# C and GpSimd's B loaded from a copy in DRAM, and the second stage's norms by transposes with VectorE's statistics

## The chip, the cores and the metric

The kernel runs on one core of a Trainium2 chip. The metric is the device time of the whole program in microseconds, the median of several runs; one more execution is profiled, and every busy time and wait below is from that one. A core has five engines that work through their own instruction streams in order and wait for each other by semaphores: TensorE (PE, with its weight loads shown apart as PEld), VectorE (DVE), ScalarE (ACT), GpSimd (POOL) and SyncE (SP), which here issues nearly all DMA transfers.

## The reference

Four layers follow each other on an image batch x of shape (4, 192, 64, 64), all in float32. Layers 0 and 1 hold the selective scans, and are what the change concerns:

```python
# layer 0: tokens = 4096 rows of 192 values per image
xs = layernorm(x); out = xs + mamba1(xs) + mamba2(flip(xs, channels))
# layer 1: t = layernorm over channels of each position
x1 = x + mamba(t);  x2 = x1 + gelu(batchnorm(depthwise3x3(x1)))
out = x2 + mlp(layernorm(x2))            # 192 -> 768 -> gelu -> 192

def mamba(x):                            # d = 384 inner channels, n = 16 states
    xc, z = split(x @ in_w.T)
    xc = silu(causal_conv(xc))
    dt, B, C = split(xc @ x_w.T)         # 12, 16 and 16 values per token
    dt = softplus(dt @ dt_w.T + dt_b)
    h[t] = exp(dt[t] * A) * h[t-1] + (dt[t] * xc[t]) * B[t]     # for each d and n
    y[t] = sum_n h[t] * C[t] + D * xc[t]
    return (y * silu(z)) @ out_w.T
```

Layer 2 is a depthwise convolution with weights made from the image's means, layer 3 a window transformer with a 16-fold structured product. The change leaves both alone.

## The kernel before, in words

The program has three stages. `two_mambas` does layer 0 (to about 5160 us), `mamba_block` layer 1 (to about 8480 us), `conv_and_windows` layers 2 and 3. In the first two stages an image is cut into 8 tiles of T = 512 tokens, 32 tiles in all. A mamba on a tile is 12 groups k of 4 scans j: the 384x16 states lie as 48 pieces of 128 partitions (16 channels by 8 states), and each piece is one scan of 512 steps on VectorE. Stage one has two mambas a tile, so 96 scans; stage two one, so 48.

For each group, `load` (L598) brings dt and dt*xc from DRAM, each row repeated over 8 partitions (dtE and dtxE, 4 transfers of 256 KB each). `product` (L635) multiplies dtxE by B: VectorE for most groups, with B in PSUM, and GpSimd for the groups named `shared`, with a copy Bs of B in SBUF. `decay` (L647) makes dA = exp(dtE * A) on ACT into one of three PSUM banks, two scans ahead. `step` (L653) is the scan on VectorE. `read` (L664) keeps the last state and multiplies h by C on GpSimd. `sum` (L672) adds over the states by four matmuls on TensorE.

B and C are needed with each of their 16 rows repeated over the partitions. In the kernel before this is a matmul of the tile `dbl` (the 44 values per token) with a matrix of ones (`Expand.spread`): `spread` (L607) for B, `spread_C` (L616) for C, whose result ACT copies to SBUF (L630), as it copies B for GpSimd (Bs). C0 has one buffer in stage two (`alone`), otherwise C has two; Bs has one.

Around the scans stands everything else of a tile. `front` (L464) is the input projection, the convolution, `dbl` (L496), dt, and the writes of dt and dt*xc to DRAM (`r_dt`, `r_dtx`, L520). In stage two, `norm` is the layernorm before it, `back` (L1076) the output projection with the residual into `strip`, `tail` (L1120) the 3x3 convolution (ps_dw), a Gelu, an addition and a second layernorm, and `end` the MLP. These are generators in five lanes of `Behind` (L176). Once per scan, `tick` lets lanes emit a `Piece` each, as far as its declared cost fits: `pe` against a budget of TensorE time per scan, `act` against one of ACT time, `bank` against two PSUM banks, `after` against flags, `wait` against a number of scans, `burst` only where VectorE is about to do a product (long ACT operations with a table load), `lock` one norm at a time. `later` emits an evacuation one to three scans after its matmul. So the order on each engine is fixed when the program is built, by the planner's counts, and the engines then run as semaphores let them. Tiles' `norm` runs two tiles ahead of the scan, `front` one tile ahead, `tail` one or two behind.

The second stage's norms (`NormT.run`, L303) work with channels in partitions. A matmul with a matrix of 1/192 gives the mean in every partition, VectorE subtracts it (L310), ACT squares (L317), 8 matmuls with one output column each give the variance (L322), ACT and GpSimd make the reciprocal root (L333, L334), 4 matmuls spread it (L340), VectorE multiplies (L348), and ACT applies gain and shift (L355).

All transfers named here are issued from SP's queue in program order. Each waits there for its source, for its buffer to be free, and for an older transfer, and holds those behind it.

Of the kernel before, what the change touches and what calls it, by code (L numbers as in the profile page):

```python
# [286 lines left out]
class NormT:  # L287


    FIRST = dict(pe=1.7, bank=True)  # L290

    def __init__(self, nc, const, work, behind):
        self.nc, self.work, self.behind = nc, work, behind
        self.mean_w = const.tile([CP, CP], F32, name="mean_w")
        nc.vector.memset(self.mean_w, 1.0 / C)
        self.eps = const.tile([128, 1], F32, name="eps")
        nc.vector.memset(self.eps, EPS)
        self.minus_half = const.tile([128, T // 128], F32, name="minus_half")
        nc.vector.memset(self.minus_half, -0.5)
        self.ident = const.tile([128, 128], F32, name="ident")  # L300
        make_identity(nc, self.ident)

    def run(self, x, g, b, d, which):  # L303
        nc, behind = self.nc, self.behind
        nq = T // 128
        mean = behind.bank([CP, T], "mean")
        for k in range(2):
            nc.tensor.matmul(mean, self.mean_w, x[:, k, :], start=(k == 0), stop=(k == 1))
        h = behind.later(
            lambda: nc.vector.tensor_tensor(  # L310
                d, x, mean.unsqueeze(1).broadcast_to([CP, 2, T]), ALU.subtract
            ),
            dve=True,
        )
        yield Piece(after=[h], wait=3, act=1.05, lock=True)
        sq = self.work.tile([CP, 2, T], F32, name="ln_sq", bufs=1)
        nc.scalar.activation(sq, d, AF.Square)  # L317
        yield Piece(2.5, wait=2, bank=True)
        var = behind.bank([128, nq], "var")
        for q in range(nq):  # L320
            for k in range(2):
                nc.tensor.matmul(  # L322
                    var[:, q : q + 1],
                    sq[:, k, bass.ts(q, 128)],
                    self.mean_w[:, 0:1],
                    start=(k == 0),
                    stop=(k == 1),
                )
        behind.locked = False
        rs = self.work.tile([128, nq], F32, name="ln_rs", tag=f"ln_rs{which}", bufs=1)  # L330

        def power():
            nc.scalar.activation(rs, var, AF.Identity, bias=self.eps)  # L333
            nc.gpsimd.tensor_tensor(rs, rs, self.minus_half, ALU.pow)  # L334

        h = behind.later(power, act=0.25)
        yield Piece(1.3, after=[h], wait=4, bank=True)
        rb = behind.bank([CP, T], "rb")
        for q in range(nq):
            nc.tensor.matmul(  # L340
                rb[:, bass.ts(q, 128)],
                rs[:, q : q + 1].to_broadcast([128, CP]),
                self.ident,
                start=True,
                stop=True,
            )
        h = behind.later(
            lambda: nc.vector.tensor_tensor(  # L348
                d, d, rb.unsqueeze(1).broadcast_to([CP, 2, T]), ALU.mult
            ),  # L350
            dve=True,
        )
        for k in range(2):
            yield Piece(after=[h], wait=0 if k else 3, act=0.8)
            nc.scalar.activation(  # L355
                d[:, k, :], d[:, k, :], AF.Identity, scale=g[:, k : k + 1], bias=b[:, k : k + 1]
            )
# [49 lines left out]
class Expand:  # L407
# [5 lines left out]
    def __init__(self, nc, const, spread_ap, gather_ap):  # L413
        self.spread = const.tile([KX, 4, 128], F32, name="spread")
        nc.sync.dma_start(self.spread, spread_ap)
        self.gather = const.tile([128, 2, 32], F32, name="gather")
        nc.sync.dma_start(self.gather, gather_ap)


class Mamba:  # L420
# [43 lines left out]
    def front(self, xn, first, u):  # L464
# [26 lines left out]
        yield Piece(2.6, bank=True, wait=2 if self.summed else 4)  # L491
# [6 lines left out]
        for d in range(ND):  # L498
            yield Piece(0.85, bank=True, after=[h], wait=0 if d else 3)
            if d == 0:  # L500
                dt = self.work.tile([128, ND, 1 + T if self.summed else T], F32, name="dt", bufs=1)
                dt = dt[:, :, :T]
                dtx = raw[:, :, K - 1 :]
# [103 lines left out]
    def spread(self, u, o):  # L607

        B = u["B", o] = self.psum_a.tile([128, T], F32, name=f"B{o}", bufs=1)
        self.nc.tensor.matmul(B, self.ex.spread[:, o, :], u["dbl"], start=True, stop=True)  # L610

# [4 lines left out]
    def spread_C(self, u, o):  # L616

        both = [("Bs", 0, 1)] if any(k % 2 == o for k in self.shared) else []
        both.insert(len(both) if self.summed else 0, ("C", 2 + o, 1 if self.alone(o) else 2))
        for n, i, bufs in both:  # L620
            if n == "C":
                yield Piece(0.85, bank=True, wait=3 * self.alone(o))
            v = self.work.tile([128, T], F32, name=f"{n}{o}", bufs=bufs)
            if n == "C":
                ps = self.behind.bank([128, T], f"ps_{n}")
                self.nc.tensor.matmul(ps, self.ex.spread[:, i, :], u["dbl"], start=True, stop=True)
            else:
                ps = u["B", o]
            done = self.behind.later(
                lambda v=v, ps=ps: self.nc.scalar.copy(v, ps), bank=(n == "C")  # L630
            )
            yield Piece(after=[done])
            u[n, o] = v

# [75 lines left out]
class Scans:  # L710
# [6 lines left out]
    def __init__(self, nc, units, behind):  # L717
        self.nc, self.units, self.behind = nc, units, behind
        self.due = {}
        for n, unit in enumerate(units):  # L720
# [3 lines left out]
            unit[1]["z_free"] = [units[n - 2][1]["gated"]] if n > 1 else []  # L724

# [287 lines left out]
def mamba_block(tc, x, p96, p96_ap, p128, p128_ap, m_in, ex_aps, out, sums, following):  # L1013
# [4 lines left out]
    with ExitStack() as ctx:  # L1018
# [50 lines left out]
        def norm(u):  # L1069
            xn = u["xn"] = scan.tile([CP, 2, T], F32, name="xn", bufs=1)  # L1070
            yield from ln.run(u["x"], w["ln1_g"], w["ln1_b"], xn, 1)
# [48 lines left out]
        def tail(b, t):  # L1120
# [37 lines left out]
            yield Piece(1.7, bank=True, wait=4, after=[taken[0]])  # L1158
            xn = work.tile([CP, 2, T], F32, name="xn2", tag="xn2", bufs=1)
            yield from ln.run(x2, w["ln2_g"], w["ln2_b"], xn, 2)  # L1160
            units[b * NT + t]["past"][0] = True
            taken[0] = [False]
            behind.add(3, end(b, t, x2, xn, taken[0]), Piece(1.7, bank=True, wait=2))
# [28 lines left out]
        def before(n):  # L1192
            if n + 1 < len(units):
                behind.add(1, front(units[n + 1]), Piece())
            if n + 2 < len(units):
                behind.add(1, norm(units[n + 2]), Piece(1.7, bank=True, after=[units[n + 2]["loaded"]]))

        def after(n):
# [3 lines left out]
            first = [u["done"]] + ([units[n - 3]["ended"]] if n > 2 else [])  # L1202
            for t2 in ([t - 1] if t else []) + ([t] if t == NT - 1 else []):
                behind.add(2, tail(b, t2), Piece(2.6, bank=True, after=first, wait=2))
# [7 lines left out]
        behind.add(1, norm(units[0]))  # L1212
        behind.add(1, front(units[0]), Piece())
        behind.add(1, norm(units[1]))
# [523 lines left out]
def scan_matrices():  # L1738
    spread = np.zeros((KX, 4, 16, 8), np.float32)
    for o in range(4):  # L1740
        for n in range(8):
            spread[RK + 8 * o + n, o, :, n] = 1.0
# [4 lines left out]
    return spread.reshape(KX, 4, 128), gather.reshape(128, 2, 32)  # L1747
# [100 lines left out]
```

## Time and profile before

| | |
|---|---|
| median of 3 runs | 10454.71 us (10451.56 to 10456.62) |
| profiled execution, its time | 10458.36 us |
| its span | 10456.3 us |
| granted TensorE clock, mean | 0.87 |
| busy over the span: PE, DVE, ACT, POOL | 81%, 84%, 64%, 76% |
| DMA | 1515.56 MB, mean 145 GB/s |
| L655, scans on VectorE | 4608, 1.27 us each |
| L668, L642, GpSimd's products with C and Bs | 1152 and 320, 4.53 and 4.58 us each |
| L630, ACT's copies of C and Bs | 192 and 128, 0.58 and 0.59 us each |
| L626, matmuls for C | 384 records, 223.6 us |
| L308, L322, L340, matmuls of the norms | 148.4, 140.1, 81.9 us |

Times are microseconds from the start of the span. A busy time is the time in which an engine worked on instructions of a group; the idle time beside it is that just before them, with the engine and line whose work ended it. Idle time of an engine that sets no pace costs nothing. A float32 matmul of this kernel leaves two records, a transpose one. Matmuls overlap, so their mean duration is longer than the share of busy time of each.

### The profile page before, as it was taken

The numbers are of one execution on the slowest core, as the hardware profiler recorded it, in microseconds if no ns is written. First come the engines' busy times: TensorE is split into PE (matmuls) and PEld (weight loads), VectorE is DVE, ScalarE is ACT, GpSimd is POOL, SyncE is SP. The second block draws the span as 40 slices with busy tenths as digits, with TensorE's granted clock in tenths as the row PEclk, the third lists the DMA queues.
The fourth block names the chain that finished last, engine by engine and source line by source line (L and its number), as shares of the span: only waits on it lengthen the run. The fifth ranks groups of instructions, "written<-read, shape, count | busy, mean of one in ns | idle before, by whom it ended". The sixth has DMA issues, their size and how long they took to land. (4 is left out here: it accounts for less than half of the span.)

```text
span 10456.3 us, 96737 instructions
## 1 busy us (share of the span) xinstructions
PE 8434.2 (81%) x30648; PEld 3477.0 (33%) x30648; DVE 8762.8 (84%) x7569; ACT 6672.4 (64%) x9690; POOL 7925.1 (76%) x3712
## 2 busy tenths in 40 slices
PE   6777777777777777777658898888898886989898
PEld 2222322222222222222223333333333333545455
DVE  7999999999999999999958888888888876555552
ACT  5777777767766767677646777777777753444433
POOL 6999999999999999999959888888888861101100
PEclk8888888888888888888768899999999997999999
DMA  6666666666666666666645555555555543122110
GB/s 166 177 183 185 181 182 182 182 179 182 184 183 179 182 185 183 179 183 185 160 120 154 150 141 151 146 151 147 146 156 139 152 109 74 44 61 53 41 41 19
DMA packets 969737, 1515.56 MB, mean 145 GB/s; under 512 B 244308, under 2 KB 277280, under 8 KB 968712
## 3 DMA queue, kind: packets, MB, share of 16 engines
q1 hardware_dynamic: 968224, 1506.06, 54.7%
q8 instruction: 243, 3.98, 0.2%
q10 hardware_dynamic: 1000, 3.30, 0.1%
q14 instruction: 270, 2.21, 0.1%
HBM read 1295.91 MB, written 213.12 MB: 144 GB/s over the span
## 5 line engine op out<-in xcount | busy, mean ns | idle before, releaser
L655 DVE TENSOR_TENSOR_SCAN h<-dA,m_state,h 128x512 f32<-128x512 f32 x3328 | 4040.0, 1266 | 219.9 <-ACT dA L649 157.6
L649 ACT ACTIVATE dA<-dtE,m_A 128x512 f32<-128x512 f32 x4608 | 3103.8, 686 | 1236.2 <-DVE h L655 939.8
L668 POOL TENSOR_TENSOR h<-h,C 128x2048 f32<-128x2048 f32 x832 | 3768.6, 4530 | 71.2 <-ACT C L630 3.7
L642 DVE TENSOR_TENSOR h<-dtxE,B 128x2048 f32<-128x2048 f32 x832 | 1882.4, 2262 | 79.1 <-DMA dtxE<-r_dtx 69.0
L655 DVE TENSOR_TENSOR_SCAN h_apart<-dA,m_state,h_apart 128x512 f32<-128x512 f32 x1280 | 1551.6, 1263 | 143.8 <-ACT dA L649 136.7
L642 POOL TENSOR_TENSOR h_apart<-dtxE,Bs 128x2048 f32<-128x2048 f32 x320 | 1464.7, 4577 | 20.5 <-ACT dA L649 10.7
L668 POOL TENSOR_TENSOR h_apart<-h_apart,C 128x2048 f32<-128x2048 f32 x320 | 1449.5, 4530 | 25.8
L677 PE MATMUL y<-h,gather 128*32 128x512 f32 x6656 | 1040.9, 702 | 428.4 <-POOL h L668 242.8
L1383 POOL TENSOR_TENSOR d<-d,rs 128x512 f32<-128x512 f32 x64 | 86.4, 1350 | 1596.2 <-DVE rs L1382 1576.1
L476 PE MATMUL ps_in<-xT,m_in_w 96*128 96x512 f32 x1536 | 951.6, 772 | 340.2 <-ACT o L919 213.4
L558 PE MATMUL ps_conv<-raw,m_conv 128*128 128x512 f32 x1536 | 724.3, 601 | 25.8 <-ACT raw L483 19.0
L476 PEld LDWEIGHTS ps_in<-xT,m_in_w 96*128 96x128 f32 x1536 | 365.6, 248 | 933.3 <-issue 372.7
L494 PE MATMUL ps_x<-xc,m_pack 128*68 128x512 f32 x576 | 374.8, 802 | 213.3 <-ACT xc L490 198.6
L1132 PE MATMUL ps_dw<-strip,dw 96*96 96x512 f32 x1152 | 544.8, 620 | 1.3 <-ACT x L1141 0.9
L677 PE MATMUL y<-h_apart,gather 128*32 128x512 f32 x2560 | 395.5, 694 | 171.9 <-POOL h_apart L668 161.1
L505 PE MATMUL ps_dt<-dbl,m_dt_w 68*128 68x512 f32 x576 | 379.3, 761 | 167.6 <-ACT dbl L496 101.3
L677 PEld LDWEIGHTS y<-h,gather 128*32 128x32 f32 x6656 | 140.3, 115 | 1072.1 <-issue 574.0
L1548 PE MATMUL sed_ps<-xn,sed 64*128 64x256 f32 (+3 forms) x2944 | 486.1, 403 | 7.0 <-DVE y L1567 7.0
L476 PE MATMUL ps_in<-xn,m_in_w 96*128 96x512 f32 x768 | 393.8, 647 | 118.2 <-ACT z L483 65.0
L396 PE MATMUL ps_o<-hid,t 128*96 128x512 f32 x768 | 412.9, 676 | 76.6 <-ACT C L630 69.2
L515 POOL TENSOR_TENSOR raw<-dt,xc 128x1536 f32<-128x1536 f32 x96 | 324.8, 3384 | 176.6 <-ACT dt L514 130.5
L649 ACT ACT_TABLE_LOAD x345 | 442.6, 1283 | 14.7 <-DMA dtE<-r_dt 8.6
(200 smaller groups left out, 11998.0 us busy)
## 6 DMA issues: line engine op xcount, KB each, us to landing
dtE<-r_dt SPq DMA_DIRECT2D x2304, 256.0 KB, 5.3
dtxE<-r_dtx SPq DMA_DIRECT2D x2304, 256.0 KB, 4.4
r_dt<-dt SPq DMA_DIRECT2D x96, 768.0 KB, 4.0
r_dtx<-raw SPq DMA_DIRECT2D x96, 768.0 KB, 6.5
x<-x SPq DMA_DIRECT2D x64, 384.0 KB, 3.6
img<-x SPq DMA_DIRECT2D x28, 512.0 KB, 9.1
xt<-in_x SPq DMA_DIRECT2D x32, 384.0 KB, 5.2
x<-o SPq DMA_DIRECT2D x32, 384.0 KB, 3.8
```

The costliest lines, as they stand in the source:

```text
L396: nc.tensor.matmul(ps, self.w2[:, m, bass.ts(k, CP)], h[:, m, :], start=(m == 0), stop=(m == NH - 1),)
L476: nc.tensor.matmul(ps, self.in_w[:, k, bass.ts(e, 128)], xn[:, k, :], start=(k == 0), stop=(k == 1))
L494: nc.tensor.matmul(ps, self.x_w[:, d, :], xc[:, d, :], start=(d == 0), stop=(d == ND - 1))
L505: nc.tensor.matmul(ps, self.dt_w[:, bass.ts(d, 128)], dbl, start=True, stop=True)
L558: nc.tensor.matmul(ps, self.conv[:, d, j, :], raw[:, d, j : j + T], start=(j == 0), stop=(j == K - 1))
L642: engine.tensor_tensor(h, u["rows", k // 2, 1], u[B, k % 2].unsqueeze(1).broadcast_to([128, 4, T]), ALU.mult)
L649: self.nc.scalar.activation(dA, u["rows", k // 2, 0][:, j, :], AF.Exp, scale=self.A[:, k, j : j + 1])
L655: self.nc.vector.tensor_tensor_scan(h[:, j, :], u.pop(("dA", k, j)), h[:, j, :], self.state[:, k, j : j + 1], ALU.mult, ALU.add,)
L668: nc.gpsimd.tensor_tensor(h, h, u["C", k % 2].unsqueeze(1).broadcast_to([128, 4, T]), ALU.mult)
L677: self.nc.tensor.matmul(u["ys"][32 * j : 32 * j + 32, :], self.ex.gather[:, i // 2, :], h[:, j, :], start=(i == 0), stop=(i == 3 and self. ...
L1132: nc.tensor.matmul(ps, dw[:, k, j, :], s[:, k, dy : dy + rows, dx : dx + HW], start=(j == 0), stop=(j == 8),)
L1548: nc.tensor.matmul(out, sed[p, int(h is not None), i ^ position(k, s), cols], xn[b, g][p, c, :], start=group(t) not in begun, stop=left[gr ...
```

## The change

- `front` writes the 32 rows of B and C of `dbl` to DRAM (`r_bc`), just before the dt projection.
- `spread_C` no longer uses TensorE, PSUM or ACT: C and Bs come by one transfer each of 256 KB from `r_bc`, in which every row is read 16 times. B for VectorE stays a matmul into PSUM. The matrix `spread` shrinks from four parts to two.
- A flag `spread`, set when the second half of B is spread, now holds the next `dbl` back (`dbl_free`).
- `NormT.run` turns the tile around: 8 transposes on TensorE to tokens in partitions (ln_t), two copies on ACT (ln_xs), `bn_stats` and `bn_aggr` for four groups of 128 tokens on VectorE, four small operations on GpSimd (with the reciprocal root), four scalings on ACT, 8 transposes back (ln_b), and gain and shift on ACT as the evacuation. The output tile is taken only at the transposes back, by the function `to`; the wait for the MLP before (`taken`) moves there too. The lock is taken with the first piece and kept to the last transposes.
- The tail waits for the end of the MLP two tiles before its own tile, written so that it also holds at an image's last tile.

```diff
 class NormT:
-    FIRST = dict(pe=1.7, bank=True)
+    FIRST = dict(pe=0.5, bank=True, lock=True)
...
-    def run(self, x, g, b, d, which):
...
+    def run(self, x, g, b, to, which, after=()):
+        nc, behind, ident = self.nc, self.behind, self.ident
         nq = T // 128
...
+        xs = self.work.tile([128, nq, C], F32, name="ln_xs", bufs=1)
+        made = []
+        for part in range(0, nq, 2):
+            if part:
+                yield Piece(0.5, bank=True)
+            ps = behind.bank([128, 2, C], "ln_t")
+            for q in range(2):
+                for k in range(2):
+                    nc.tensor.transpose(
+                        ps[:, q, bass.ts(k, CP)], x[:, k, bass.ts(part + q, 128)], ident[:CP, :CP]
+                    )
+            made.append(
+                behind.later(lambda part=part, ps=ps: nc.scalar.copy(xs[:, part : part + 2, :], ps), act=0.5)
+            )
+        yield Piece(after=made, wait=3)
...
+        for q in range(nq):
+            nc.vector.bn_stats(sums[:, q].rearrange("p a b -> p (a b)"), xs[:, q, :])
+        for q in range(nq):
+            nc.vector.bn_aggr(mv[:, q, :], sums[:, q].rearrange("p a b -> p (a b)"))
+        yield Piece(wait=1)
+        nc.gpsimd.tensor_scalar(rs, mv[:, :, 1], EPS, None, ALU.add)
+        nc.gpsimd.tensor_tensor(rs, rs, self.minus_half, ALU.pow)
+        nc.gpsimd.tensor_tensor(shift, mv[:, :, 0], rs, ALU.mult)
+        nc.gpsimd.tensor_scalar(shift, shift, -1.0, None, ALU.mult)
+        yield Piece(wait=3)
+        for q in range(nq):
+            yield Piece(act=0.55)
+            nc.scalar.activation(
+                xs[:, q, :], xs[:, q, :], AF.Identity, scale=rs[:, q : q + 1], bias=shift[:, q : q + 1]
+            )
         for k in range(2):
...
+            yield Piece(0.5, bank=True, wait=0 if k else 2, after=after)
+            out = out if k else to()
+            ps = behind.bank([CP, T], "ln_b")
+            for q in range(nq):
+                nc.tensor.transpose(ps[:, bass.ts(q, 128)], xs[:, q, bass.ts(k, CP)], ident)
+            h = behind.later(
+                lambda k=k, ps=ps, out=out: nc.scalar.activation(
+                    out[:, k, :], ps, AF.Identity, scale=g[:, k : k + 1], bias=b[:, k : k + 1]
+                ),
+                act=0.75,
+            )
         behind.locked = False
...
+        yield Piece(after=[h])
@@ front
-        yield Piece(2.6, bank=True, wait=2 if self.summed else 4)
+        yield Piece(2.6, bank=True, wait=2 if self.summed else 4, after=u["dbl_free"])
...
             if d == 0:
+                bc = u["bc"] = self.dram.tile([2 * NS, T], F32, name="r_bc", bufs=3)
+                nc.sync.dma_start(bc, dbl[RK : RK + 2 * NS, :])
@@ spread
+        u["spread"][0] = o == 1
@@ spread_C
-        both.insert(len(both) if self.summed else 0, ("C", 2 + o, 1 if self.alone(o) else 2))
-        for n, i, bufs in both:
-            if n == "C":
-                yield Piece(0.85, bank=True, wait=3 * self.alone(o))
+        both.insert(len(both) if self.summed else 0, ("C", NS, 1 if self.alone(o) else 2))
+        for n, at, bufs in both:
+            if n == "C" and self.alone(o):
+                yield Piece(wait=4)
             v = self.work.tile([128, T], F32, name=f"{n}{o}", bufs=bufs)
-            if n == "C":
-                ps = self.behind.bank([128, T], f"ps_{n}")
-                self.nc.tensor.matmul(ps, self.ex.spread[:, i, :], u["dbl"], start=True, stop=True)
-            else:
-                ps = u["B", o]
-            done = self.behind.later(
-                lambda v=v, ps=ps: self.nc.scalar.copy(v, ps), bank=(n == "C")
-            )
-            yield Piece(after=[done])
+            rows = u["bc"][at + 8 * o : at + 8 * o + 8, :]
+            self.nc.sync.dma_start(v, rows.unsqueeze(0).broadcast_to([16, 8, T]))
             u[n, o] = v
+            yield Piece()
@@ tail
-            yield Piece(1.7, bank=True, wait=4, after=[taken[0]])
-            xn = work.tile([CP, 2, T], F32, name="xn2", tag="xn2", bufs=1)
-            yield from ln.run(x2, w["ln2_g"], w["ln2_b"], xn, 2)
+            yield Piece(wait=4, **ln.FIRST)
...
+            yield from ln.run(x2, w["ln2_g"], w["ln2_b"], to, 2, [taken[0]])
@@ after
-            first = [u["done"]] + ([units[n - 3]["ended"]] if n > 2 else [])
             for t2 in ([t - 1] if t else []) + ([t] if t == NT - 1 else []):
+                old = b * NT + t2 - 2
+                first = [u["done"]] + ([units[old]["ended"]] if old >= 0 else [])
                 behind.add(2, tail(b, t2), Piece(2.6, bank=True, after=first, wait=2))
```

## The prediction

> **What bounds the kernel now.** I read the page's slices first: 3 stages, the first to about 5160 us (32 tiles of 512 tokens, two scans each), the second to about 8480 us (32 tiles, one scan), then the windows, which the change does not touch. Then busy time by window. The columns are the window and its length, then PE, weight loads, DVE, ACT, POOL, then the granted clock, the DMA share and GB/s:
>
> ```profile
> 1000.00:4900.00 3900.00, 2997.32 (x9987) 1095.80 (x9986) 3783.32 (x2899) 2733.68 (x4201) 3720.51 (x1585) 0.84 0.69 182
> 6000.00:8000.00 2000.00, 1781.13 (x5767) 665.31 (x5766) 1711.98 (x1382) 1446.80 (x1935) 1741.27 (x875) 0.93 0.55 147
> ```
>
> Stage one is VectorE's: 97% busy, so all that can be won there is 3%. In stage two nobody is full: TensorE 89%, GpSimd 87%, VectorE 86%, ACT 72%. Its pace is set by engines that wait for each other. So I read VectorE's waits, stage one first, then two (us in all, times, longest):
>
> ```profile
> DVE h_apart L655 <- ACT dA L649: 38.3, 24, 1.7
> DVE h L655 <- ACT dA L649: 31.8, 96, 0.5
> ...
> DVE strip L1103 <- PE ps_out L1094: 91.7, 40, 5.4
> DVE h_apart L655 <- ACT dA L649: 55.6, 48, 2.7
> DVE h L655 <- ACT dA L649: 55.3, 85, 1.5
> DVE xn L310 <- PE mean L308: 49.4, 40, 2.3
> DVE xn L348 <- PE rb L340: 23.4, 20, 2.0
> ```
>
> The window of stage two holds 944 scans of 48 a tile, so 19.67 tiles of 101.7 us: 87.0 us of VectorE's work and 14.6 idle (strip 4.7, dA 5.6, mean and rb 3.7). Upstream, from the waits of ACT and TensorE in the same window:
>
> ```profile
> ACT C L630 <- PE ps_C L626: 75.4, 20, 7.0
> ...
> ACT xn L355 <- DVE xn L348: 61.6, 37, 2.6
> ...
> PE ps_o L396 <- ACT C L630: 55.5, 17, 3.4
> ```
>
> The C copies hold ACT for 3.8 us a tile and TensorE for 2.8. The timeline of one tile shows why: ACT is in its Gelu burst of 5.3 us, its C copy is late, TensorE idles 3.4 us, comes back at half clock, and the next C is 3.6 us late.
>
> A natural experiment lies at the start of stage two, where tiles come without tail and MLP; the second line is a full tile:
>
> ```profile
> 5440.40:5533.30 92.90, 62.52 (x183) 20.46 (x182) 83.32 (x65) 57.40 (x81) 84.44 (x40) 0.72 0.60 157
> 6500.00:6601.00 101.00, 89.87 (x301) 33.24 (x300) 87.59 (x72) 74.40 (x100) 87.63 (x45) 0.95 0.57 149
> ```
>
> With TensorE at 63 us the tile still takes 92.9, and VectorE idles 9.6. Relief of TensorE is worth something, but not one for one.
>
> [...]
>
> **The change, part by part, per tile of stage two.**
>
> *C and Bs.* Removed: two spread matmuls on TensorE (L626, 48.1 us in the window, 2.4 a tile) and three copies on ACT (C and Bs at 0.58 us, 1.7 a tile). Added on SP's queue: one 64 KB write of B and C rows, behind ACT's copy of dbl, and three broadcast loads of 256 KB. The loads stand in SP's order between those of dtE and dtxE, which are issued 8 and 12 scans ahead (8 scans are 10 us and at least one product of 2.3) and land in 5.3 and 4.4 us. So about 6 us of slack covers some 0.6 us of issue for each added transfer; DMA volume grows by 0.9 MB on 15 MB a tile. The write waits for ACT's copy of dbl with loads queued behind it on SP, but is planned three scans after that copy, and SP already stands a longer wait at the same place without one of VectorE's products going short of its load:
>
> ```profile
> SPq L520 <- ACT dt L514: 168.5, 19, 10.2
> ```
>
> I take 0 for it. C0 has one buffer in stage two: its load waits for GpSimd's read of k=10, and the loads behind it on SP wait too. GpSimd still has the read of k=11 (4.53 us) before it needs C0. A 384 KB store with nothing ahead of it lands in 2.6 us, so I cost the wait at 0 to 1 us on GpSimd and take 0; without that read it would be 3 to 4.
>
> *Norms, two a tile.* TensorE loses mean 88.6, var 79.2 and rb 46.0 us in the window, 10.9 a tile, and gets 32 transposes. L880 has 192 of them in 29.8 us, 0.155 each, 5.0 a tile (its mean of 278 ns, not overlapped, would make 8.9). With C: 8.4 us less (4.4 at worst). VectorE loses two passes of 1.21 us a norm, 4.9 a tile, and gets 4 bn_stats over 192 and 4 bn_aggr. No row shows them. [...] the aggregates I set at 0.1 to 0.2 (the smallest rows here are 80 and 98 ns). [...] I take 1.9, 3.8 a tile: 1.1 less. ACT loses 1.05+0.26+2x0.81 = 2.9 a norm and gets two copies of 384 columns (0.47, between 0.31 for 192 and 0.58 for 512), four scalings (0.53, L862) and two outputs (0.76, L884): 4.6. That is 3.4 more a tile, 1.7 with the copies of C gone. GpSimd gets three small operations (0.2 each) a norm: 1.3 a tile, 88.5 to 89.8.
>
> *Waits.* Those for mean and rb go (3.7). The statistics wait for ACT's copies, but are planned three scans behind them: 0.3. The scalings come four at a time, 2.1 us of ACT in front of the next dA, which VectorE wants two scans ahead (2.5 us); against that ACT no longer stalls on C (3.8) and on xn (3.1). I take 0.4 off the dA waits (bounds 2.5 off, 3 on). The strip wait follows TensorE's lateness: 1.5 off (0 to 3.5). The lock of the norm is now held until its last transposes, so the tail's Gelu and norm stand some ten scans later in the order; the MLP after it starts within three scans of where it did, so this costs nothing. The new condition on dbl, that B of the scan before is spread, holds the front back only where it ran ahead anyway.
>
> Sum: -1.1-3.7+0.3-0.4-1.5 = -6.4, a tile of 95.3. GpSimd's floor, at the 95.4% that it carries in stage one, is 89.8/0.954 = 94.1, so the last microsecond is doubtful: I take 5.5. Over 30 full tiles 165 us.
>
> **Stage one.** 24.2 tiles of 161 us in the window; per tile, four C matmuls leave TensorE (4.3 us) and seven copies ACT (4.1 us, and ACT's wait before Bs, 166.7 us in the window, 6.9 a tile). VectorE's waits for dA are 2.9 a tile. The longest (1.6 us) comes where ACT waits for a conv matmul beside B and C. I take half, 1.4 a tile, 45 us for 32 tiles (bounds +20 and -90). Starts and drain: the same chain of eight steps in other forms, 0, give or take 10.
>
> Total: 165+45 = 210. The profiled execution took 10458.4 (span 10456.3), the median is 10454.7; I take 210 from the median: 10245.
>
> **Rivals.** *TensorE alone paces stage two*: then its 8.4 comes in full, 30x8.4+60 = 310, 10145. For it: its 89%. Against: the light tile. *GpSimd takes over*: the light tile kept 8.5 us idle on GpSimd; 89.8+8.5 = 98.3, 3.4 a tile, 100 us, and 15 in stage one: 10340. For it: the numbers just given; against: those waits were for VectorE and for a first transfer. *Slower, by the clock*: [...] Its 82 us at 0.93 become 82x0.93/clock: at 0.85 the relief is gone (90), at 0.80 it is 95, some 5 us more than now, 150 us on 30 tiles, less stage one's 45: 10560. [...] *No effect*, the idle only changing its name: 10455.
>
> **How the numbers follow.** Forecast (10195 to 10300) 0.43, TensorE alone 0.16, GpSimd 0.25, no effect 0.05, slower 0.11. The measurement can tell 0.2%, 21 us. So faster 0.84, same 0.05, slower 0.11. The range for 8 in 10 takes in the first three with their unknowns: 10115 to 10420.
>
> **What would show it.** Right: stage two's tiles at 95 to 97 us, no waits at mean or rb, the strip wait down by a third, granted clock still above 0.88, GpSimd above 92%, stage one at 159 us a tile, no GpSimd wait on the C transfers above 1 us. Wrong: dA waits in stage two above 8 us a tile (the scalings), bn_stats above 0.5 us, waits of GpSimd for C, loads of dtE late behind C0 on SP, or a clock below 0.85.

## The result, and the profile after

The changed kernel takes 10616.45 us (median; 10614.59 to 10619.01), the kernel before 10453.13 us beside it. The ratio is 1.0155 with a 95% interval of 1.0142 to 1.0168: 1.55% slower, where 2% faster was forecast. The profiled execution has a span of 10617.2 us and a mean granted clock of 0.849.

The split by stage comes from GpSimd's reads of C, of which each scan tile has twelve. The first read of stage two starts at 5307.7 us (before: 5342.9), the last tile's first read at 8628.9 us (before: 8464.8). So everything up to stage two is 35 us earlier and stage two, from the first tile's first read to the last tile's, is 199 us longer (3321 us, before 3122); what lies behind the last tile's first read, the drain and the windows, is 3 us shorter. From the sixth tile on, the tiles of stage two come 109.2 us apart; before it was about 101.

The windows of the changed kernel, in the columns of the prediction (window, length, PE, weight loads, DVE, ACT, POOL, clock, DMA share, GB/s):

```profile
1000.00:4900.00 3900.00, 2915.08 (x9829) 1096.99 (x9822) 3783.78 (x2901) 2655.38 (x4032) 3720.70 (x1587) 0.82 0.74 194
6000.00:8000.00 2000.00, 1624.02 (x4816) 564.29 (x4815) 1561.06 (x1506) 1369.91 (x1891) 1642.80 (x923) 0.87 0.55 145
```

Stage one is what it was: VectorE 97% busy, with fewer matmuls and copies beside it. In stage two *every* engine has become emptier: TensorE 81%, VectorE 78%, ACT 68%, GpSimd 82%. The window holds 18.31 tiles (before: 19.74), so per tile the work is nearly the forecast one: VectorE 86.7 to 85.3 us, ACT 73.3 to 74.8, GpSimd 88.2 to 89.7. No engine has taken over; the time is in waits. VectorE's, in the same window (us in all, times, longest):

```profile
DVE h_apart L647 <- ACT dA L641: 154.6, 55, 4.1
DVE h L647 <- ACT dA L641: 150.9, 149, 2.6
DVE strip L1100 <- PE ps_out L1091: 105.5, 36, 5.2
DVE ln_sums L325 <- ACT ln_xs L317: 15.4, 18, 0.9
```

The waits for mean and rb are gone; the new norms' wait in their place (ln_sums) is 0.8 us a tile. But the scans now wait 16.7 us a tile for dA, where it was 5.6, and the strip 5.8 us, where it was 4.6. TensorE's waits say what is upstream (ps_in is the input projection, ps_x the product that makes dbl, ps_h and ps_o the two products of the MLP, ln_b a norm's transposes back):

```profile
PE ps_in L471 <- ACT xn L346: 120.2, 19, 6.3
PE ln_b L344 <- ACT hid L377: 53.7, 19, 2.8
PE ps_x L489 <- ACT xn L346: 49.9, 18, 2.8
PE ps_h L372 <- ACT ln_xs L317: 41.2, 18, 2.3
PE ps_o L391 <- ACT ln_xs L317: 36.3, 19, 1.9
```

Each of these stands about once a tile, always behind something that ACT empties, and four of the five behind the new norms' copies and outputs. Where the tile named isn't the matmul's input (ps_x, ln_b, ps_h and ps_o), the wait is for the PSUM bank that ACT empties. The timeline of one tile shows the largest (start, duration, engine, line, what it writes and reads, how many). First ACT:

```profile
6553.74 1.28 ACT L384 ACT_TABLE_LOAD   x1
6555.04 2.76 ACT L384 ACTIVATE hid<-hid 128x3072 f32<-128x3072 f32 x1
6557.82 1.28 ACT L641 ACT_TABLE_LOAD   x1
6559.11 1.91 ACT L641 ACTIVATE dA<-dtE,m_A 128x512 f32<-128x512 f32 x3
6560.97 0.76 ACT L346 ACTIVATE xn<-ln_b,t 96x512 f32<-96x512 f32 x1
```

and TensorE around it:

```profile
6530.61 8.75 PE L372 MATMUL ps_h<-xn,t 96*128 96x512 f32 x12 [2.29 <-ACT ln_xs L317]
...
6554.90 0.55 PE L313 MATMUL ln_t<-ident,x 96*128 96x96 f32 x4
6561.78 6.81 PE L471 MATMUL ps_in<-xn,m_in_w 96*128 96x512 f32 x8 [6.33 <-ACT xn L346]
6568.52 1.06 PE L669 MATMUL y<-h,gather 128*32 128x512 f32 x8
6570.65 1.98 PE L471 MATMUL ps_in<-xn,m_in_w 96*128 96x512 f32 x4 [1.06 <-ACT xc L583]
```

The second half of xn is emptied from PSUM behind the MLP's Gelu with its two table loads and three dA. TensorE stands 6.3 us and comes back slow: 8 matmuls take 6.8 us, where the next 4 take 2.0; the clock granted from 6561.7 to 6569.0 us is 0.56, from 6569 to 6575 it is 0.99. (In the kernel before, the clock granted while the matmuls behind its stand of 3.4 us ran, from 6542.03 to 6545.50 us, is 0.50.) ACT then waits for what TensorE owes it (its wait for ps_in, ACT raw, grows from 1.9 to 4.4 us a tile). Rows of the two matmuls in the stage's window (busy us, mean ns of one, idle before them). The kernel before:

```profile
L476 PE MATMUL ps_in<-xn,m_in_w 96*128 96x512 f32 x474 | 232.9, 622 | 65.1 <-ACT z L483 36.8 <-ACT xc L586 18.0 <-DVE x L1167 9.1
L377 PE MATMUL ps_h<-xn,t 96*128 96x512 f32 x480 | 218.7, 597 | 11.1 <-ACT hid L382 11.1
```

and the changed kernel:

```profile
L471 PE MATMUL ps_in<-xn,m_in_w 96*128 96x512 f32 x444 | 274.2, 760 | 164.7 <-ACT xn L346 120.2 <-ACT z L478 24.3 <-ACT xc L583 20.1
L372 PE MATMUL ps_h<-xn,t 96*128 96x512 f32 x434 | 259.0, 752 | 41.2 <-ACT ln_xs L317 41.2
```

By busy time a tile these two rows give back 6.2 us of the 8.4 that TensorE was to lose.

### The profile page after: what moved, and what is told of

Its sections match the earlier page's. It is cut to its first block, busy times and chain, and to the rows that moved or that the text cites. A ratio compares the mean times of both kernels' runs of the same rounds, so it can differ in the third digit from the quotient of the medians.

```text
span 10617.2 us, 95491 instructions
## 1 busy us (share of the span) xinstructions
PE 8207.1 (77%) x29496; PEld 3352.3 (32%) x29496; DVE 8708.8 (82%) x7952; ACT 6609.0 (62%) x9626; POOL 7971.4 (75%) x3904
## 5 line engine op out<-in xcount | busy, mean ns | idle before, releaser
L669 PE MATMUL y<-h,gather 128*32 128x512 f32 x6656 | 992.3, 672 | 512.4 <-POOL h L660 365.8
L471 PE MATMUL ps_in<-xT,m_in_w 96*128 96x512 f32 x1536 | 923.6, 755 | 328.5 <-ACT z L478 307.0
L555 PE MATMUL ps_conv<-raw,m_conv 128*128 128x512 f32 x1536 | 696.5, 599 | 10.1 <-ACT raw L478 7.2
L471 PE MATMUL ps_in<-xn,m_in_w 96*128 96x512 f32 x768 | 477.0, 765 | 263.4 <-ACT xn L346 166.2
L489 PE MATMUL ps_x<-xc,m_pack 128*68 128x512 f32 x576 | 418.3, 885 | 203.9 <-ACT xc L485 131.9
L1129 PE MATMUL ps_dw<-strip,dw 96*96 96x512 f32 x1152 | 518.5, 599 | 1.2 <-ACT x L1138 0.9
L372 PE MATMUL ps_h<-xn,t 96*128 96x512 f32 x768 | 446.9, 736 | 78.8 <-ACT ln_xs L317 63.8
```

The source lines that it names most:

```text
L372: nc.tensor.matmul(ps, self.w1[:, k, bass.ts(m, 128)], x[:, k, :], start=(k == 0), stop=(k == 1))
L471: nc.tensor.matmul(ps, self.in_w[:, k, bass.ts(e, 128)], xn[:, k, :], start=(k == 0), stop=(k == 1))
L489: nc.tensor.matmul(ps, self.x_w[:, d, :], xc[:, d, :], start=(d == 0), stop=(d == ND - 1))
L555: nc.tensor.matmul(ps, self.conv[:, d, j, :], raw[:, d, j : j + T], start=(j == 0), stop=(j == K - 1))
L669: self.nc.tensor.matmul(u["ys"][32 * j : 32 * j + 32, :], self.ex.gather[:, i // 2, :], h[:, j, :], start=(i == 0), stop=(i == 3 and self. ...
L1129: nc.tensor.matmul(ps, dw[:, k, j, :], s[:, k, dy : dy + rows, dx : dx + HW], start=(j == 0), stop=(j == 8),)
```

## The experiments

Four explanations stood now. *Order*: the planner puts the new norms' longer chain elsewhere, and the tile pays for where things meet (the Gelu of x2 moves from scan 33 to 45, the MLP's from 45 to scan 1 of the next tile; a scan number is a place in ACT's program order, counted by the dA made). *Work*: ACT's added operations. *Clock*: the transposes lower the granted clock (0.87 in stage two's window, where it was 0.93). *Transfers*: C late on SP's queue. Tile times below are means over twenty tiles in the later part of stage two; before 101.3, changed 109.2. A kernel's time also holds what lies behind the last tile; where an order changes that, it is told apart.

### One part at a time

The transfers alone (the change without `NormT` and its callers):

> The kernel before with the transfers of C and Bs alone; both norms as they were. If the new norms are what costs (order, clock or added ScalarE work), this is faster than before: stage one keeps its 35 us, stage two is relieved of 1.7 us of ScalarE copies a tile, together 10350 to 10420 us, and the waits for dA stay near the 5.6 us a tile of before. If the transfers are to blame (C late behind a DMA wait, or Bs crowding the queue), stage two grows here too: 10550 us or more, with dA or C waits of 8 us a tile and above.

10447.39 us, ratio 0.9993 (0.9984 to 1.0001). Both expectations missed: no loss, but no relief either. The first read of stage two comes at 5311.1 us, 32 earlier, and stage two gives 20 of that back, with a tile of 102.1 us. So 2.4 us of TensorE and 1.7 us of ACT less a tile buy nothing there, in an order that is again another one (the MLP's Gelu at scan 37 in place of 45). GpSimd has no wait for C in the window. ACT waits for the dtE loads, which stand behind C0 on SP, for 13.7 us in the window, 0.7 a tile.

The new norms alone (C and Bs as before), then one norm at a time with the transfers, with the old class kept beside the new one; the two classes then share one buffer (`ln_buf`), which is an addition of these two kernels. The main lines of the edits:

> The new norms alone; C and Bs come by matmul and copy as before. If the norms cost by the work that they add to ScalarE and TensorE, stage two has at least the 109 us a tile of the changed kernel, plus the 1.7 us of copies: 10650 us or more. If they cost by the order in which the work comes, this kernel has another order (the Gelu of x2 near scan 13 to 21 and not 45), and its tile may be anything from 98 to 120 us; a number unlike 109 speaks for the order. If the transfers are to blame, it is near 10400 us.

```diff
# second norm alone: the first one as before
-            yield from ln.run(u["x"], w["ln1_g"], w["ln1_b"], to, 1)
+            yield from ln_old.run(u["x"], w["ln1_g"], w["ln1_b"], xn, 1)
# first norm alone: the second one as before
-            yield from ln.run(x2, w["ln2_g"], w["ln2_b"], to, 2, [taken[0]])
+            yield from ln_old.run(x2, w["ln2_g"], w["ln2_b"], xn, 2)
```

> C and Bs by transfers and the new norm for the second norm (x2) alone; the first norm (x) as before. The bursts stand at scans 33, 37 and 45 as in the kernel with the transfers alone (101.6 us a tile), so the new norm is compared inside the same order. If a new norm costs by itself (ScalarE on the way between two TensorE stretches[...]), half of the loss is here: 104 to 106 us a tile, 10520 to 10590 us. If only the collision with the bursts costs (the second half of xn behind the MLP's Gelu), it is at 100 to 102.5 us a tile, 10400 to 10480 us.

> The mirror image: the new norm for the first norm (x) alone, the second as before. The bursts stand at scans 1, 17 and 37. A cost of the norm by itself gives 104 to 106 us a tile, 10520 to 10590 us; a cost of the collision alone, which this order does not have (the first norm ends at scan 45, the next Gelu comes at scan 1), gives 100 to 102.5 us a tile, 10400 to 10480 us.

Both norms without the transfers: 10746.31 us, ratio 1.0279 (1.0264 to 1.0295), a tile of 110.2 us on average, between 100 and 129, and 85 us of the loss lie behind the last tile; by itself this would fit work as well as order. The second norm alone: 10730.68 us, 1.0262 (1.0246 to 1.0278), a tile of 112.1 us. The first alone: 10535.10 us, 1.0076 (1.0062 to 1.0089), 105.6 us. The loss sits with the norms, but not in parts that add: with the second norm alone the tile is *longer* than in the changed kernel, which has both. If it all belonged to the norms' work, it would have been about halved. Against its expectation, the kernel with the second norm alone isn't in the order of the transfers alone: the bursts are where they were, but the front half of the tile has moved (SiLU of xc from scan 17 to 29, dbl from 20 to 32, dt from 29 to 35). So it compares orders as well as norms. I had expected both variants on one side of 104; only the first norm alone came where a cost of its own would put it, and it does so without the collision shown above.

### The clock

> The changed kernel with its 32 transposes a tile issued as plain matmuls against the same identity, in the same order with the same data. If transposes are the reason that the granted clock sags to 0.87 in stage two (my rival that goes by the clock), the clock is back at 0.90 or more and the tile at 101 us or less: 10330 to 10400 us. If the clock sags because TensorE idles at its waits, nothing changes: 10616 us within 0.3 per cent, clock 0.87.

```diff
-                    nc.tensor.transpose(ps[...], x[...], ident[:CP, :CP])
+                    nc.tensor.matmul(ps[...], x[...], ident[:CP, :CP], start=True, stop=True)
```

10565.45 us, ratio 1.0106 (1.0091 to 1.0121), between the two expectations: 51 of the 163 us come back. The window of this kernel in stage two:

```profile
6000.00:8000.00 2000.00, 1669.85 (x5512) 651.77 (x5512) 1589.89 (x1534) 1387.33 (x1921) 1675.00 (x936) 0.91 0.56 148
```

and the row of the MLP's first matmuls in that window:

```profile
L373 PE MATMUL ps_h<-xn,t 96*128 96x512 f32 x432 | 209.8, 631 | 30.7 <-ACT ln_xs L318 30.7
```

The clock is 0.91 instead of 0.87 in the same order, and ps_h, which follows the transposes, takes 631 ns instead of 752. The plain matmuls also last longer (10.5 us a tile, where the transposes took 5.7), and the run doesn't tell apart which of the two, the kind of instruction or its length, goes with the clock. The transposes are one cause in this order; most of the loss stays.

### The order

Three kernels change one planner number and no instruction of the program (two to four of ACT's table loads fall away):

```diff
# e5: the four scalings of a norm spread out
-            yield Piece(act=0.55)
+            yield Piece(act=0.55, wait=1)
# e12: the MLP's Gelu later
-        yield Piece(after=made, burst=True, act=5.3)
+        yield Piece(after=made, wait=6, burst=True, act=5.3)
# e17: the kernel BEFORE, its second norm later
-            yield Piece(1.7, bank=True, wait=4, after=[taken[0]])
+            yield Piece(1.7, bank=True, wait=10, after=[taken[0]])
```

> The changed kernel with one more planned scan between the four scalings of a norm: no instruction is added or taken away, but the planner finds another order, in which the Gelu of x2 comes at scan 13, the MLP's at 33 and the SiLU at 45, so that the bursts stand 12 to 20 scans apart and no norm output stands behind one. If the order is what costs, waits for dA fall from 16.7 to under 9 us a tile, the tile to 95 to 101 us, the time to 10180 to 10380 us. If the added work, the transposes or the transfers cost, it stays at 10550 to 10650 us.

10643.87 us, 1.0182 (1.0165 to 1.0199): slower as a whole, with the bursts apart. Stage two itself is 40 us shorter than in the changed kernel (3281 us), and what lies behind the last tile's first read is 64 us longer, with one more MLP left for it. But the tile is still 107.9 us and VectorE's waits for dA are 19.3 us a tile, more than before the edit, so setting the bursts apart is not the remedy that my first form of the theory made it. The same number also moved SiLU of xc, dbl and dt by 6 to 15 scans, so spacing was not tested alone. In this order TensorE stands before the sums over states for GpSimd's read, 13.6 us a tile, a wait that the changed kernel doesn't have. One line from TensorE's waits in e5, two from VectorE's:

```profile
PE y L669 <- POOL h L660: 252.5, 34, 9.2
...
DVE h L647 <- ACT dA L641: 219.9, 63, 9.1
DVE h_apart L647 <- ACT dA L641: 138.4, 54, 5.5
```

> The changed kernel with six planned scans more ahead of the MLP's Gelu, and nothing else: the planner then finds an order with the Gelu of x2 at scan 21, the MLP's at 37, SiLU at 45 and the second norm at scans 27 to 41. If the collision costs, the tile is 100 to 103 us and the kernel 10330 to 10450 us. If any order pays for the new norms, as the run with the scalings spread already did (108.3 us a tile), it is 106 us a tile or more, 10550 us or more.

10495.22 us, 1.0037 (1.0023 to 1.0051): 121 of the 163 us are back. In stage two it is 160 of the 199 us; 37 us are lost behind the last tile, where one more MLP is left. The tile of 102.8 us is the one expected; the time is above the range by what is lost at the end, and because the tiles from the sixth to the twelfth still take about 105. The number moves more than the one Gelu: the Gelu of x2 and the second norm stand elsewhere too, as the expectation says. The window of e12:

```profile
6000.00:8000.00 2000.00, 1665.62 (x5074) 585.44 (x5072) 1646.23 (x1589) 1434.33 (x1985) 1737.35 (x969) 0.87 0.58 153
```

and VectorE's waits in it:

```profile
DVE h L647 <- ACT dA L641: 116.1, 95, 4.4
DVE x L1169 <- PE ps_o L391: 83.5, 36, 7.4
DVE strip L1100 <- PE ps_out L1091: 79.0, 22, 6.8
DVE h_apart L647 <- ACT dA L641: 62.4, 56, 4.5
```

The waits for dA fall from 16.7 to 9.2 us a tile and the strip's from 5.8 to 4.1; a wait for the MLP's output ps_o comes in, 4.3 us a tile. The granted clock is the same 0.87 as in the changed kernel, so this gain comes without a higher clock.

> The kernel before with ten planned scans in place of four ahead of its second norm, and nothing else: the planner then puts the MLP's Gelu at scan 1, as in the changed kernel, the Gelu of x2 at 37 and SiLU at 45. The work is that of before to the instruction. If the order alone can cost what the change cost, 104 to 112 us a tile: 10540 to 10790 us. If the order costs only together with the new norms, within 1 us of 101.1 us a tile: 10430 to 10490 us.

10724.99 us, 1.0259 (1.0244 to 1.0274): 270 us lost with the same work. About 175 of them lie in stage two, with a tile of 108.7 us, and about 100 behind the last tile's first read, again with one more MLP left. The window of e17:

```profile
6000.00:8000.00 2000.00, 1738.79 (x5334) 646.27 (x5332) 1603.18 (x1296) 1342.13 (x1791) 1621.84 (x810) 0.89 0.53 138
```

and VectorE's waits in it:

```profile
DVE h L655 <- ACT dA L649: 192.6, 87, 6.6
DVE h_apart L655 <- ACT dA L649: 81.3, 95, 3.9
DVE strip L1103 <- PE ps_out L1094: 64.6, 20, 4.4
```

The picture is that of the changed kernel (all engines emptier, dA waits of 14.9 us a tile, a clock of 0.89), made from the old work. So the order alone can cost stage two nearly what the change did. This kernel also moves the output projection from scan 13 to 29 and SiLU of xc, dbl and dt by 6 to 13 scans, so it isn't the changed kernel's order; it shows the size of the lever.

### The same edits in two orders

Four edits leave the changed kernel's program order as it is and move work between engines.

> The changed kernel, in the same program order, with GpSimd taken out of the chain of a norm: VectorE adds epsilon and forms the shift; the power of minus one half is left out, so the norms divide by nothing and the output is another. In the changed kernel ScalarE's scalings wait 2.7 us a tile for GpSimd's shift, and GpSimd stands at 90 us a tile. If the hand-offs of the norm's chain between engines that issue in order are what stretches the tile, taking two of them away gives 1 to 3 us a tile back: 10510 to 10590 us. If the order of the bursts alone decides, or TensorE's clock, nothing moves: 10600 to 10630 us.

> The changed kernel, in the same program order, with the four scalings of a norm as VectorE instructions (four times about 0.3 us a norm) in place of ScalarE's (1.85 us a norm). If the work added to ScalarE is what costs, 3.7 us a tile leave its order and the tile falls by 3 to 4 us: 10490 to 10530 us. If the clock or the hand-offs between TensorE and ScalarE cost, at most 1 us a tile: 10580 to 10620 us.

> The changed kernel, in the same program order, with all four PSUM banks of a norm (both of the first transposes, both of the second) emptied by VectorE instead of ScalarE. In the changed kernel TensorE waits 11 us a tile behind banks and inputs that ScalarE empties (6.5 us of it for the second half of xn, which stands behind the MLP's Gelu on ScalarE). If this hand-off is what costs, TensorE no longer waits there, the clock comes back to 0.90 or more and the tile to 102 us or less: 10380 to 10440 us. If the added work costs, 4.6 us a tile leave ScalarE, much like moving the scalings: 10470 to 10530 us. If the transposes' clock costs, 10560 to 10620 us.

> Both together: the banks emptied and the scalings made by VectorE, in the changed kernel's program order, so that a norm has no ScalarE instruction. If ScalarE is where the norms cost, by work or by hand-offs, stage two is at 96 to 101 us a tile and the kernel at 10200 to 10400 us, faster than before. If the clock under transposes costs, the tile stays above 104 us and the kernel above 10500 us, with a clock below 0.90.

```diff
# e7: scalings on VectorE
-            nc.scalar.activation(xs[:, q, :], xs[:, q, :], AF.Identity, scale=rs[...], bias=shift[...])
+            nc.vector.tensor_scalar(xs[:, q, :], xs[:, q, :], rs[...], shift[...], ALU.mult, ALU.add)
# e8: the norm's PSUM banks emptied by VectorE
-                nc.scalar.copy(xs[:, part : part + 2, :], ps)
+                nc.vector.tensor_copy(xs[:, part : part + 2, :], ps)
-                nc.scalar.activation(out[:, k, :], ps, AF.Identity, scale=g[...], bias=b[...])
+                nc.vector.tensor_scalar(out[:, k, :], ps, g[...], b[...], ALU.mult, ALU.add)
```

| edit | us | ratio to before | tile |
|---|---|---|---|
| e6, no GpSimd in the norm, and no power of minus one half | 10710.32 | 1.0244 (1.0227 to 1.0261) | 111.8 |
| e7, scalings on VectorE | 10747.78 | 1.0280 (1.0265 to 1.0295) | 112.4 |
| e8, banks emptied by VectorE | 10567.41 | 1.0108 (1.0093 to 1.0123) | 105.8 |
| e9, e7 and e8 | 10747.64 | 1.0280 (1.0264 to 1.0295) | 110.9 |

Taking work from ACT or GpSimd made three of four slower. e6 and e7 missed both of their ranges on the slow side. e8 and e9 fell into the ranges that I had put down for the clock. That doesn't show the clock as the cause: e9 is 131 us slower than the changed kernel at a clock of 0.88, above its 0.87. The timeline of e7 shows why the price was not the one I had put down:

```profile
6030.14 5.45 DVE L336 TENSOR_SCALAR ln_xs<-ln_xs,ln_rs,ln_shift 128x192 f32<-128x192 f32 x4 [0.72 <-POOL ln_shift L332]
6030.32 4.57 POOL L660 TENSOR_TENSOR h<-h,C 128x2048 f32<-128x2048 f32 x1
6035.51 4.79 DVE L647 TENSOR_TENSOR_SCAN h_apart<-dA,m_state,h_apart 128x512 f32<-128x512 f32 x4
```

Four scalings, 0.37 us each at the median, take 5.45 us: one of them begins beside a GpSimd read of 4.57 us and ends just after it, and the scans stand behind them. VectorE's busy time rises by more than 9 us a tile. e6 has the same in two of its small operations on 4 columns, below. Emptying PSUM on VectorE has no such stretch (in e8 the norm's outputs take 779 to 806 ns), and gains 49 us. The added work on ACT is thus not refuted as a cost by e7, whose replacement cost more than it freed; e8 takes 4.3 us a tile off ACT and gets 3.4 back, but only in this order, as the next table shows.

The edit that gained and the transposes' edit, now inside e12's order:

> The kernel with the later Gelu (102.4 us a tile), with plain matmuls against the identity in place of the norms' transposes; same order. If transposes cost by the clock wherever they stand, it gains what it gained in the changed kernel, 2 us a tile: 10430 to 10445 us. If they cost there only because TensorE had idled beside them, nothing or a loss by the added TensorE work (the matmuls take longer than transposes): 10490 to 10530 us.

> The kernel with the later Gelu, with the norm's four PSUM banks emptied by VectorE; same order. In it TensorE still waits 5 us a tile at the first transposes of the second norm behind ScalarE's xn. If that hand-off is a cost of its own, 2 to 3 us a tile: 10405 to 10440 us. If the order decides what a hand-off costs, anything between 10440 and 10560 us.

> Both edits inside the better order. If both causes are their own and add, 4 to 5 us a tile: 97.5 to 98.5 us, 10350 to 10375 us, and this beats every kernel so far. If they share the same waits, 10400 to 10440 us. If neither holds in this order, above 10480 us.

| edit | in the changed kernel's order | in e12's order |
|---|---|---|
| none | 10616.45, 1.0155 (1.0142 to 1.0168) | 10495.22, 1.0037 (1.0023 to 1.0051) |
| plain matmuls | 10565.45, 1.0106 (1.0091 to 1.0121) | 10488.86, 1.0035 (1.0022 to 1.0048) |
| banks by VectorE | 10567.41, 1.0108 (1.0093 to 1.0123) | 10583.71, 1.0122 (1.0105 to 1.0139) |
| both | not run | 10592.39, 1.0131 (1.0116 to 1.0146) |

The plain matmuls raise the clock again, from 0.87 to 0.90, and this time it is worth nothing that can be told apart:

```profile
6000.00:8000.00 2000.00, 1712.55 (x5700) 675.76 (x5703) 1656.82 (x1592) 1444.14 (x1991) 1740.60 (x973) 0.90 0.59 154
```

Emptying by VectorE gains 49 us in one order and loses 88 us in the other. Neither has a price of its own; what each is worth depends on the order that it stands in.

### What is worth keeping

> The kernel before with the transfers of C and Bs in the first stage alone; the second stage is the one before, instruction for instruction. Stage one keeps the 32 to 35 us that it gained (first read of stage two at 5308 and not 5343 us), stage two keeps its 101.1 us a tile: 10415 to 10430 us, ratio 0.997, faster than both. If part of that gain came from how stage two fills, 10440 to 10455 us.

The kernel before with the transfers in stage one alone (the new code under `if not self.summed`) takes 10434.76 us, ratio 0.9980 (0.9973 to 0.9987): faster than the kernel before by 0.2% and than the changed kernel, though between my two ranges. The first read of stage two comes at 5319.0 us, 24 earlier than before, and stage two keeps its tile of 101.3.

## Why the prediction was wrong, step by step

- *The step that failed*: "the tail's Gelu and norm stand some ten scans later in the order; the MLP after it starts within three scans of where it did, so this costs nothing." The shift was seen and costed at nothing without asking what the moved pieces would meet. The MLP's Gelu moved by four scans, in front of the second half of xn, and TensorE's wait there is 120 us in the window, 6.6 a tile. With the same work in another order (e12) 160 of the 199 us lost in stage two came back; an order changed alone (e17) cost the old kernel 175 us there. Which of the moves in e12 did it is not told apart.
- *The dA waits*, "0.4 off (bounds 2.5 off, 3 on)": 11.1 us a tile on. The bounds weighed the scalings against the stalls that ACT loses, not TensorE and ACT making each other late. Waits above 8 us were on the list of what would show the forecast wrong.
- *The strip*, "1.5 off": 1.2 on, from the same lateness of TensorE.
- *TensorE, 8.4 us less*: the removed and added instructions are as listed (the transposes take 5.7 us a tile, where 5.0 was taken), but busy time fell from 90.2 to 88.7 only, since ps_in and ps_h take 6.2 us a tile more, behind waits and, as e4 shows for ps_h (631 ns with plain matmuls, 752 with transposes), behind transposes.
- *Right*: VectorE's work (1.4 less, forecast 1.1), ACT's (1.5 more, 1.7), GpSimd's (1.5 more, 1.3), bn_stats (0.35 us; the bound was 0.5), the mean and rb waits (2.9 us off net, forecast 3.4), no GpSimd wait for C in the window. The 1.9 us a norm for the statistics was my estimate, with no row of bn_stats or bn_aggr behind it; the two take 56.8 us of VectorE's busy time for the 37 norms of the window, 1.5 each. With dA and strip the sum closes: -1.4-2.9+11.1+1.2 = 8.0, and the tile grew by 7.9.
- *Stage one*: the tile hardly moved. From the second tile on it takes 160.4 us before and 160.3 after, not 159, and VectorE's waits for dA fell by 5 us in 3900; "I take half" was too much. Of the 35 us by which stage two starts earlier, 17.5 are in the first tile (179.4 to 161.9 us; VectorE's waits for dA between 80 and 280 us fall from 20.3 to 6.3) and 15 between the last tile's first read and stage two's. These are the starts and drains that the forecast had at 0, give or take 10. So that 35 is near the 45 forecast is luck.
- *The rival by the clock* has a share in the loss (e4: 0.91 instead of 0.87, and 51 us), but not its point of decision. That transposes go with a lower clock was an assumption that no run had shown by then. By its own sum TensorE's 82 us become 88 at the measured 0.87, less than before, and yet the kernel lost; e12 is almost as fast as before at the same 0.87, and e14 shows a clock regained for no time. That its 10560 lies near the measured 10616 is luck.
- *The floor* of 94.1 us never came into play: no engine was near its limit.

Open: which property of an order sets the tile. Setting the bursts apart didn't mend it. Three of the slow orders (e5, e17 and the second norm alone) have SiLU of xc at scan 29, where before, the changed kernel and e12 have it at 17; whether that costs was not tried. Across these kernels slow tiles come with dA waits, but e9 has few (4.4 us a tile) and 110.9 us, with VectorE 90% busy instead. A kernel with the new norms in exactly the old order was not tried, so what their own work costs isn't known: in e12 stage two is still 39 us longer than before.

## What to carry to other kernels

In a stage where no engine is full, the sum of the work added and removed does not forecast the time: a change that moves pieces in an in-order program must be followed to what each moved piece lands in front of, on each engine that it visits. Before crediting or blaming an operation, change the order once without touching the work; here one planner number moved stage two by 160 and by 175 us, as much as everything the change was about. Look at what is left behind the last tile as well: another order moved 37 to 100 us there. An edit tried in one order may have the other sign in the next.

## What the runs showed of the hardware

- In e6 and e7 small tensor_scalar and tensor_tensor operations of VectorE from SBUF to SBUF became long beside GpSimd's instructions. A 128x192 scaling of e7 takes 366 ns at least, 369 at the median and 4589 at most. The mean of 1362 ns is about what one long one in four gives (my estimate from these figures), and the timeline of four above has one. Two operations on 128x4 in e6 have medians of 1.9 and 2.1 us, while a third of the same size behind them took 0.17. In e6's timeline of one norm the first two end 0.02 to 0.03 us after a GpSimd instruction that began before them, and the third stands where GpSimd is idle:

```profile
6002.16 4.51 POOL L659 TENSOR_TENSOR h<-h,C 128x2048 f32<-128x2048 f32 x1
...
6004.78 1.92 DVE L329 TENSOR_SCALAR ln_rs<-ln_mv 128x4 f32<-128x4 f32 x1
...
6006.63 1.26 POOL L698 TENSOR_TENSOR xc<-xc,z 128x512 f32<-128x512 f32 x1
6006.73 1.18 DVE L330 TENSOR_TENSOR ln_shift<-ln_mv,ln_rs 128x4 f32<-128x4 f32 x1
...
6007.94 0.17 DVE L331 TENSOR_SCALAR ln_shift<-ln_shift 128x4 f32<-128x4 f32 x1
```

The norm's outputs, which VectorE makes from PSUM in e8, stay within 779 to 806 ns, and in e7 bn_stats stays within 333 to 362 ns and the scans have means of 1.26 and 1.27 us. Why the small operations became long was not shown. The scaling of e7 (count, then minimum, median and maximum in ns):

```profile
L336 DVE TENSOR_SCALAR ln_xs<-ln_xs,ln_rs,ln_shift x143: 366/369/4589, 6030.1 to 7998.3; 128x192 f32<-128x192 f32 x143
```

and the product for the shift in e6:

```profile
L330 DVE TENSOR_TENSOR ln_shift<-ln_mv,ln_rs x36: 1178/2091/2999, 6006.7 to 7955.2; 128x4 f32<-128x4 f32 x36
```

- A granted clock raised from 0.87 to 0.91 (e4) or to 0.90 (e14) by the same edit went with a gain of 51 us in one order and nothing measurable in the other.
